# Graph stage in fewer tiles: block sums on VectorE, norms on GpSimd, and a permutation in two-byte parts

## The chip, the cores and the metric

One core of one Trainium2 chip runs the whole program in one launch. The metric is the device time in microseconds (us). Times of one instruction are in nanoseconds (ns). The engines are TensorE (PE, with its weight loads as PEld), VectorE (DVE), ScalarE (ACT), GpSimd (POOL) and SyncE (SP, here a queue for transfers).

## The reference

There are 32 graphs (B) of 512 nodes (N) with 64 features (D). Each passes through four steps with a residual and a normalisation after each. Cut to what matters:

```python
def reference(x, adj, nodemask, ...):
    # layer 0: messages = (A / clip(deg, 1)) @ x
    # layer 1: Chebyshev polynomials of the Laplacian, 4 orders, then a weight and a bias
    # layer 2: hyperbolic attention over all pairs of nodes (logmap, sigmoid, expmap, proj)
    # layer 3: dilate the adjacency, then for each node and feature a weighted
    #          sum of the 0.25, 0.5 and 0.75 quantiles over its neighbours,
    #          then a two-layer perceptron
    # between the layers: x = layernorm(x + layer(x)); a node mask of ones
    return x
```

The third layer is the unusual one: for each node, the values of its neighbours must be sorted, feature by feature. A node has at most 24 neighbours in the case that the fast path covers (K = 24).

## The kernel before, in words

**Lanes.** A graph goes through lanes: `front` (load, transposition of the adjacency, layers 0 and 1), `pairs` and `tail` (layer 2), `graph` (dilation, order of the nodes by their number of neighbours, and for each neighbour its slot), `gather` (one-hot matrices on DVE, with which PE picks neighbour values into sorting strips), `sort` (a sorting network on DVE over the strips `SB` and `SH`, then the weighted sum of ranks), and `head` (for each pair of graphs: the rest of the sort, the permutation back, layer 3's perceptron, the last norm and the store).

**The order.** The program records every operation with a planned duration and a lag (`seq.op`), and a planner, `Order.issue`, lays them out in time: each lane has a due time in units of a period of 80 us (`STAGES`), the ready operation with the earliest due time goes first, and on PE a change of matmul shape is weighed by `STAY`. The result is one fixed order for each engine. Where the plan leaves PE idle, filler matmuls (`stay_active`, L1453 and L1454) are put in to keep PE active. On the chip each engine takes its list in order and waits at each instruction for what it needs. `gp` is the helper for a small operation on POOL; it plans 1.0 us and a lag of 0.5. `rsqrt` raises to the power -0.5 on POOL (L722).

**The graph stage.** `graph` builds `nbT` (neighbours, f16, 128x2048), counts, and from it `v` and then `V`, all in the pool `gm` with one buffer each. `order` ranks the nodes, builds the permutation `perm` (L852, in the buffer of `nbT`), multiplies V by it into `VP` (L857, in the buffer of `v`), and forms prefix sums over the four row blocks of VP: block j takes j+1 matmuls (L863), 10 in all, and the column totals take 4 more (L867). All matmuls are recorded by one helper, line 502; DVE's by lines 448 (two tensors), 452 (tensor and scalars) and 455; ACT's by line 483. PSUM tiles of one lane come from `bank`, and the lane `graph` has one.

**The norms.** `layernorm` runs `bn_stats` and `bn_aggr` for four blocks on DVE (L714, L717), then variance plus epsilon, the power on POOL, an offset on DVE, and four ACT instructions that scale. It is called four times per graph: twice in `front`, once at the end of `tail` (on `v`, giving `x3`), and once in `dense` at the end of `head`.

**The permutation back.** `sort` and `head` leave the weighted sums in `ap` (f32, 128x512 for a pair of graphs). `finish` multiplies it by one-hot matrices `PT` in f32, which PE takes in two passes each: eight passes per graph. The last pair of graphs has its one-hot matrices made early (`spots`).

Of the kernel before, what the change touches and what calls it, by code (L numbers as in the profile page):

```python
# [8 lines left out]
F32 = mybir.dt.float32  # L9
# [11 lines left out]
P = 128  # L21
# [10 lines left out]
K = 24  # L32
# [148 lines left out]
class Order:  # L181
# [5 lines left out]
    HOP = 0.1  # L187
    STAY = 51.0

# [214 lines left out]
def tile_adj_resnorm(ctx: ExitStack, tc: tile.TileContext, x, adj, nodemask, w1k, b1k, att_w, att_b,  # L404
# [42 lines left out]
    def tt(out, a, b, op):  # L447
        vec(lambda: nc.vector.tensor_tensor(out, a, b, op=op), out, [a, b])  # L448
# [8 lines left out]
    def cp(out, a):  # L457
        vec(lambda: nc.vector.tensor_copy(out, a), out, [a], True)
# [7 lines left out]
    def gp(f, out, ins):  # L466

        seq.op("POOL", 1.0, 0.5, f, [out], ins)

# [140 lines left out]
    nc.vector.memset(tiny, 1e-36)  # L610
    onesb = const.tile([P, P], BF16, name="onesb")
    nc.vector.memset(onesb, 1.0)
    zero = const.tile([P, 2 * P], BF16, name="zero")
    nc.vector.memset(zero, 0.0)
# [104 lines left out]
    def rsqrt(v, name):  # L719

        y = col(name)
        seq.op("POOL", 0.8, 0.6, lambda: nc.gpsimd.tensor_tensor(y, v, mhalf, op=OP.pow), [y], [v])  # L722
        return y

    def layernorm(dst, z):

        st = seq.tile(pools["small"], [P, T, nc.vector.BN_STATS_DIM], F32, "st", 2)
        mv = seq.tile(pools["small"], [P, T, nc.vector.BN_AGGR_DIM], F32, "mv", 2)
        for t in range(T):
            bn_stats(st[:, t, :], z[:, t, :])  # L730
        for t in range(T):
            bn_aggr(mv[:, t, :], st[:, t, :])
        var = col("var")
        ts(var, mv[:, :, 1], EPS, None, op0=OP.add)
# [95 lines left out]
    def order(b, res):  # L830
# [17 lines left out]
        rkh = seq.tile(pools["keep"], [P, T], F16, "rkh", 8)  # L848
        cp(rkh, rk)
        perm = seq.tile(gm, [P, T, N], F16, "perm", 1, "nbT")  # L850
        for t in range(T):
            ts(perm[:, t, :], iotap, rk[:, t:t + 1], None, op0=OP.is_equal)  # L852
        VP = seq.tile(gm, [P, T, N], F16, "VP", 1, "v")
        for j in range(T):
            pt = bank()
            for t in range(T):
                mm(pt, V[:, t, j * P:(j + 1) * P], perm[:, t, :], start=(t == 0), stop=(t == T - 1))  # L857
            act(VP[:, j, :], pt, AF.Copy)
        slot = seq.tile(pools["keep"], [P, T, N], F16, "slot", 2)
        for j in range(T):  # L860
            pt = bank()
            for k in range(j + 1):
                mm(pt, UC[:, :P] if k == j else UC[:, P:2 * P], VP[:, k, :], start=(k == 0), stop=(k == j))  # L863
            act(slot[:, j, :], pt, AF.Copy)
        pt = bank()
        for k in range(T):
            mm(pt, onesP, VP[:, k, :], start=(k == 0), stop=(k == T - 1))  # L867
        if b % 2 == 0:
# [13 lines left out]
    def front(b, res):  # L882
# [38 lines left out]
        R = seq.tile(mid, [P, T, KO * D], F32, "R", 1)  # L921
        layernorm(R[:, :, :D], z)


        dm = col("dm")
        ts(dm, deg, 2e-35, None, op0=OP.max)
        dsc = rsqrt(dm, "dsc")
        pos = col("pos")
        ts(pos, deg, 0.0, None, op0=OP.is_gt)
        tt(dsc, dsc, pos, op=OP.mult)  # L930
        g = col("g")
# [22 lines left out]
        for t in range(T):  # L954
            mm(pt[:, t, :], onesb, bias1, start=True, stop=False)
            for u in range(nu):
                mm(pt[:, t, :], RT[:, u, t * P:(t + 1) * P], wk[:, u, :], start=False, stop=(u == nu - 1))

        FL = FLS[:, b % 2]
        var, rs = layernorm(FL[:, :, :D], pt[:, :, :D])  # L960
        tt(FL[:, :, D + 2:D + 7:4], pt[:, :, D:], bc(rs, 2), op=OP.mult)

# [6 lines left out]
    def pairs(b, res):  # L969
# [128 lines left out]
        q = rowsum(x2, S, "xs")  # L1098
        stt(s1, q, -2.0, s1, op0=OP.mult, op1=OP.add)
        tt(s1, s1, hh, op=OP.mult)  # L1100
        u = wide("u")
# [168 lines left out]
    def head(b, res):  # L1270
# [19 lines left out]
        for g in range(2):  # L1290
            mm(pt[P - CUT:, g * P:(g + 1) * P], PRS[:, g:g + n - 1:2], identf, start=True, stop=True)
        act(ap[P - CUT:, :, 1, :], pt[P - CUT:, :2 * P].rearrange("p (g c) -> p g c", g=2), AF.Copy)
        for g in range(2):
            finish(b - 1 + g, res["ends"][g], ap[:, g], res["spots"][g] if b == B - 1 else None)

    def spots(ends):
# [3 lines left out]
        home = seq.tile(mid, [P, 4, N], F32, "ends", 1, "Q")  # L1300
        ones = [seq.tile(mid, [P, 4, N], F32, f"ones{g}", 1, tag) for g, tag in enumerate(("EX", "RW"))]
        seq.lane = "tail"
# [12 lines left out]
    def finish(b, end, ap, spot):  # L1315
        rk, x3 = end
        if spot:
            ones, home = spot
            po = bank(home=home and "pairs")
            for u in range(2):  # L1320
                for h in range(2):
                    mm(po[h * D:(h + 1) * D, :], ap[:, u, h * D:(h + 1) * D], ones[:, 2 * h + u], start=(u == 0),
                       stop=(u == 1 and h == 1), pair=True)
# [11 lines left out]
        for u in range(2):  # L1335
            PT = seq.tile(pools["fin"], [P, 2, N], F32, "PT", 1)
            for h in range(2):
                onehot(PT[:, h, :], rr, nposc[:, 2 * h + u:2 * h + u + 1], pools["fin"])
            for h in range(2):
                mm(po[h * D:(h + 1) * D, :], ap[:, u, h * D:(h + 1) * D], PT[:, h, :], start=(u == 0),  # L1340
                   stop=(u == 1 and h == 1), pair=True)
        for t in range(T):
# [3 lines left out]
    def dense(po, x3T, x3, dst, nm, home=None):  # L1346
# [14 lines left out]
        for t in range(T):  # L1361
            mm(py[:, t, :], onesb, bias2, start=True, stop=False)
            mm(py[:, t, :], hT[:, t * P:(t + 1) * P], w2s, start=False, stop=True)
# [6 lines left out]
    flag = const.tile([1, 1], I32, name="flag")  # L1370
    limits = const.tile([B, 2, K + 1], F32, name="limits")
    for s in range(K + 1):
# [11 lines left out]
    def within_bounds():  # L1384
# [17 lines left out]
        for i, op in enumerate((OP.is_gt, OP.is_lt)):  # L1402
# [11 lines left out]

    STAGES = {"front": (-0.6, -0.5), "pairs": (1.2, 1.3), "tail": (0.2, 1.5), "graph": (0.9, 1.0), "gather": (2.7, 2.9),
              "sort": (4.5, 4.6), "head": (4.7, 5.6), "ends": (4.0, 4.5), "check": (3.4, 4.8)}

    nc.scalar.preload_act_table_set("natural_log_exp_and_others")
    with ExitStack() as fast:
# [31 lines left out]
        def stay_active():  # L1451
            if seq.open:
                return nc.tensor.matmul(PA[:, 2 * P:], zero[:, :P], zero, start=False, stop=False)  # L1453
            return nc.tensor.matmul(PA[:, 2 * P:], identb, UC[:, :2 * P], start=True, stop=True)  # L1454
# [250 lines left out]
```

## Time and profile before

| | |
|---|---|
| time, median of 3 runs | 2621.71 us (2621.48 to 2628.53) |
| profiled execution | 2622.02 us, span 2620.2 us |
| granted TensorE clock | 0.982 |
| busy: PE, DVE, ACT, POOL | 2458.2, 2402.7, 1879.2, 815.8 us |
| chain that ended last | DVE 72%, PE 18%, ACT 6%, issue 2%, POOL 2% |
| transfers | 49.96 MB, 19 GB/s over the span |

The span runs from the first to the last instruction. "Busy" is the time in which at least one instruction of the engine runs; PE's includes the filler. A group's row gives line, engine, operation, tile written and tiles read, shapes and count, then busy time in us and mean duration in ns, then the idle time of the engine just before and what ended it. A wait's row gives the waiting instruction, the releaser, total us, times, and the longest.

### The profile page before, as it was taken

The numbers are of one execution on the slowest core, as the hardware profiler recorded it, in microseconds if no ns is written. First come the engines' busy times: TensorE is split into PE (matmuls) and PEld (weight loads), VectorE is DVE, ScalarE is ACT, GpSimd is POOL, SyncE is SP. The second block draws the span as 40 slices with busy tenths as digits, with TensorE's granted clock in tenths as the row PEclk, the third lists the DMA queues.
The fourth block names the chain that finished last, engine by engine and source line by source line (L and its number), as shares of the span: only waits on it lengthen the run. The fifth ranks groups of instructions, "written<-read, shape, count | busy, mean of one in ns | idle before, by whom it ended". The sixth has DMA issues, their size and how long they took to land.

```text
span 2620.2 us, 55667 instructions
## 1 busy us (share of the span) xinstructions
PE 2458.2 (94%) x19641; PEld 1635.4 (62%) x19667; DVE 2402.7 (92%) x9002; ACT 1879.2 (72%) x4406; POOL 815.8 (31%) x1783
## 2 busy tenths in 40 slices
PE   7999999999999999999999999999999999999997
PEld 6666566666666666666656666566666666666655
DVE  3668998999999999999999999999999999998996
ACT  5666677767777777767777677777777778776761
POOL 1233332332343333322333233333323333332210
PEclk9999999999999999999999899999999999998999
DMA  1100000000000000000000000000000000000000
GB/s 38 33 23 21 17 14 15 25 22 23 18 11 22 20 25 21 24 17 13 20 21 25 19 19 13 20 23 22 26 19 13 18 19 26 19 11 3 5 7 8
DMA packets 119723, 49.96 MB, mean 19 GB/s; under 512 B 53740, under 2 KB 119436, under 8 KB 119436
## 3 DMA queue, kind: packets, MB, share of 16 engines
q1 hardware_dynamic: 118272, 46.15, 6.4%
q8 instruction: 156, 2.56, 0.4%
q14 instruction: 131, 1.07, 0.1%
q10 hardware_dynamic: 1164, 0.18, 0.0%
HBM read 37.93 MB, written 8.39 MB: 18 GB/s over the span
## 4 chain that ended last, share of the span: by engine, by line
DVE 72%; PE 18%; ACT 6%; issue 2%; POOL 2%; DMA 0%; ACTq 0%; DVEq 0%
DVE SB L448 17%; DVE SH L448 8%; DVE gather_oh L452 6%; PE front_bank L502 5%; DVE pairs_Q L448 4%; PE gather_bank L502 3%; PE graph_bank L502 3%; DVE pairs_RW L448 3%; PE pairs_bank L502 3%; DVE sort_prod L448 3%; DVE pairs_Wt L455 3%; DVE pairs_L L455 2%; DVE tail_v L448 2%; DVE pairs_EX L448 2%; DVE pairs_RW L455 2%
## 5 line engine op out<-in xcount | busy, mean ns | idle before, releaser
L448 DVE TENSOR_TENSOR SB<-SB 128x448 f32<-128x448 f32 (+11 forms) x1424 | 565.8, 424 | 12.2 <-ACT SB L483 0.7
L502 PE MATMUL gather_bank<-gather_oh,tail_x3h 128*64 128x448 f16 (+5 forms) x5376 | 516.5, 321 | 4.8 <-ACT SB L483 3.4
L502 PEld LDWEIGHTS <-tail_x3h 128*64 128x64 bf16 x5376 | 296.0, 111 | 214.3 <-issue 112.8
L448 DVE TENSOR_TENSOR SH<-SH 128x32 f32<-128x32 f32 (+11 forms) x1744 | 347.4, 246 | 8.1
L502 PE MATMUL pairs_bank<-pairs_FT 67*128 67x512 f32 (+7 forms) x768 | 316.9, 516 | 18.7 <-ACT pairs_EX L483 7.1
L452 DVE TENSOR_SCALAR gather_oh<-graph_slot 128x256 f16<-128x256 f16 (+9 forms) x864 | 252.3, 337 | 25.3 <-PE gather_bank L502 23.5
L502 PE MATMUL front_bank<-front_AT,front_y 128*64 128x512 f32 x768 | 189.5, 607 | 18.5 <-DVE front_y L448 17.0
L502 PEld LDWEIGHTS pairs_bank<-pairs_FT 67*128 67x128 f32 (+1 forms) x768 | 130.2, 194 | 83.2 <-issue 19.7
L502 PE MATMUL graph_bank<-graph_perm,graph_V 128*128 128x512 f16 x512 | 141.0, 382 | 16.1 <-DVE graph_perm L452 13.8
L502 PEld LDWEIGHTS <-graph_nbT 128*128 128x128 f16 x1536 | 113.1, 99 | 57.6 <-issue 17.3
L722 POOL TENSOR_TENSOR front_rs<-front_var,mhalf 128x4 f32<-128x4 f32 x64 | 83.4, 1303 | 201.8 <-DVE front_var L452 152.9
L502 PEld LDWEIGHTS front_bank<-XA,front_AT 128*128 128x128 f32 x1024 | 126.0, 194 | 13.6 <-issue 6.3
L1453 PE MATMUL PA<-zero 128*128 128x256 bf16 x973 | 132.9, 278 | 0.1
L502 PE MATMUL pairs_bank<-FLS,pairs_Wt 128*128 128x66 f32 x1024 | 124.7, 274 | 3.9 <-DVE pairs_Wt L455 3.8
L502 PEld LDWEIGHTS pairs_bank<-FLS,pairs_Wt 128*128 128x128 f32 x1024 | 120.6, 192 | 10.9 <-DVE pairs_Wt L455 7.8
L502 PE MATMUL front_bank<-XA,front_AT 128*128 128x65 f32 x1024 | 124.5, 274 | 0.0
L448 DVE TENSOR_TENSOR pairs_RW<-pairs_RW,pairs_EX 128x640 f32<-128x640 f32 x128 | 104.1, 815 | 18.7 <-ACT pairs_RW L483 18.4
L502 PEld LDWEIGHTS <-tabs 128*128 128x128 f16 x1296 | 78.3, 100 | 64.2 <-issue 54.9
L502 PEld LDWEIGHTS front_bank<-front_AT,front_y 128*64 128x64 f32 x768 | 54.5, 137 | 95.6 <-issue 63.0
L483 ACT ACTIVATE graph_VP<-graph_bank 128x512 f16<-128x512 f32 x128 | 75.5, 590 | 53.7 <-PE graph_bank L502 49.4
L483 ACT ACTIVATE SB<-gather_bank 128x448 f32<-128x448 f32 (+2 forms) x192 | 81.3, 438 | 43.4 <-PE gather_bank L502 43.0
L502 PE MATMUL head_bank<-head_PT,sort_ap 128*64 128x512 f32 x240 | 111.2, 608 | 0.1
(354 smaller groups left out, 6569.8 us busy)
## 6 DMA issues: line engine op xcount, KB each, us to landing
front_A<-in_adj_dram SPq DMA_DIRECT2D x128, 256.0 KB, 2.7
XA<-in_x_dram SPq DMA_DIRECT2D x32, 128.0 KB, 2.2
xs<-tail_x SPq DMA_DIRECT2D x32, 128.0 KB, 1.9
out_dram<-head_zo SPq DMA_DIRECT2D x31, 128.0 KB, 2.0
out_dram<-tail_ends SPq DMA_DIRECT2D x1, 128.0 KB, 2.1
wk<-in_L_gnn_weight_dram ACTq DMA_DIRECT2D x1, 64.0 KB, 3.0
w1s<-in_L_gnn_W_dram ACTq DMA_DIRECT2D x2, 32.0 KB, 2.0
attw<-in_L_gnn_att_W_dram ACTq DMA_DIRECT2D x2, 0.2 KB, 3.2
```

The source lines that it names most:

```text
L448: vec(lambda: nc.vector.tensor_tensor(out, a, b, op=op), out, [a, b])
L452: vec(lambda: nc.vector.tensor_scalar(out, a, s1, s2, op0=op0, **kw), out, [a], True, (s1, s2))
L455: vec(lambda: nc.vector.scalar_tensor_tensor(out, a, s, b, op0=op0, op1=op1), out, [a, b], False, (s,))
L483: 0.3, lambda: nc.scalar.activation(out, a, f, scale=scale, **kw), [out, accum_out], [a, after] + sc, table)
L502: return nc.tensor.matmul(out, w, a, start=start, stop=stop)
L722: seq.op("POOL", 0.8, 0.6, lambda: nc.gpsimd.tensor_tensor(y, v, mhalf, op=OP.pow), [y], [v])
L1453: return nc.tensor.matmul(PA[:, 2 * P:], zero[:, :P], zero, start=False, stop=False)
```

## The change

It has these parts:

- `perm` stands in the buffer of `v`, and `VP` is written over `V` by column blocks, each seen as four strips of 128.
- The prefix sums over blocks are running sums on DVE (`sums`, three additions per graph, in the buffers of `junk` and of VP's own first blocks), so that block j takes at most two matmuls and the totals one.
- `layernorm` has a second form, the default, in which everything between `bn_stats` and the scaling runs on POOL; the two calls in `front` pass `soon=True` and keep the old form.
- Six or so small operations in `front`, `order` and `tail` move from DVE to POOL.
- `ap` is split into three bf16 parts whose sum it is (`aph`), the one-hot matrices are f16, and the permutation takes 12 two-byte matmuls per graph.
- The bias matmuls use the f16 ones instead of bf16 ones, the filler's moving operand is a broadcast column, and `limits` is f16.
- The planner's figures change: `STAY`, `STAGES`, the planned cost of `gp` and of `rsqrt`.

```diff
-    STAY = 51.0
+    STAY = 48.0
...
-        seq.op("POOL", 1.0, 0.5, f, [out], ins)
+        seq.op("POOL", 0.28, 0.25, f, [out], ins)
...
-    onesb = const.tile([P, P], BF16, name="onesb")
-    nc.vector.memset(onesb, 1.0)
-    zero = const.tile([P, 2 * P], BF16, name="zero")
+    zero = const.tile([P, P], BF16, name="zero")
...
-        seq.op("POOL", 0.8, 0.6, lambda: nc.gpsimd.tensor_tensor(y, v, mhalf, op=OP.pow), [y], [v])
+        seq.op("POOL", 1.1, 0.3, lambda: nc.gpsimd.tensor_tensor(y, v, mhalf, op=OP.pow), [y], [v])
...
-    def layernorm(dst, z):
+    def layernorm(dst, z, soon=False):
+        if not soon:
+            st = seq.tile(pools["small"], [P, T, nc.vector.BN_STATS_DIM], F32, "st", 2)
+            for t in range(T):
+                bn_stats(st[:, t, :], z[:, t, :])
+            off, even, var, d, odd, v = (st[:, :, i] for i in range(6))
+            gtt(d, even, odd, op=OP.subtract)
+            gtt(var, var, v, op=OP.add)
+            gts(d, d, 0.5, None, op0=OP.mult)
+            gts(var, var, 1.0 / D, EPS, op0=OP.mult, op1=OP.add)
+            gtt(d, d, d, op=OP.mult)
+            gtt(v, var, d, op=OP.add)
+            rs = rsqrt(v, "rs")
+            gtt(off, even, odd, op=OP.add)
+            gts(off, off, -0.5, None, op0=OP.mult)
+            gtt(off, off, rs, op=OP.mult)
+            for t in range(T):
+                act(dst[:, t, :], z[:, t, :], AF.Identity, bias=off[:, t:t + 1], scale=rs[:, t:t + 1])
+            return
...
-        cp(rkh, rk)
-        perm = seq.tile(gm, [P, T, N], F16, "perm", 1, "nbT")
+        gts(rkh, rk, 1.0, None, op0=OP.mult)
+        perm = seq.tile(gm, [P, T, N], F16, "perm", 1, "v")
...
-        VP = seq.tile(gm, [P, T, N], F16, "VP", 1, "v")
+        VP = [V[:, :, j * P:(j + 1) * P] for j in range(T)]
...
-            act(VP[:, j, :], pt, AF.Copy)
+            act(VP[j], four(pt), AF.Copy)
...
+        sums = [None, VP[0], four(seq.tile(gm, [P, N], F16, "sums", 1, "junk")), VP[0], VP[1]]
...
-            for k in range(j + 1):
-                mm(pt, UC[:, :P] if k == j else UC[:, P:2 * P], VP[:, k, :], start=(k == 0), stop=(k == j))
+            mm(four(pt), UC[:, :P], VP[j], start=True, stop=(j == 0))
+            if j:
+                mm(four(pt), UC[:, P:2 * P], sums[j], start=False, stop=True)
+                tt(sums[j + 1], sums[j], VP[j], op=OP.add)
...
-        for k in range(T):
-            mm(pt, onesP, VP[:, k, :], start=(k == 0), stop=(k == T - 1))
+        mm(four(pt), onesP, sums[T], start=True, stop=True)
...
-        layernorm(R[:, :, :D], z)
+        layernorm(R[:, :, :D], z, True)
...
-        ts(dm, deg, 2e-35, None, op0=OP.max)
+        gts(dm, deg, 2e-35, None, op0=OP.max)
...
-        ts(pos, deg, 0.0, None, op0=OP.is_gt)
-        tt(dsc, dsc, pos, op=OP.mult)
+        gts(pos, deg, 0.0, None, op0=OP.is_gt)
+        gtt(dsc, dsc, pos, op=OP.mult)
...
-        stt(s1, q, -2.0, s1, op0=OP.mult, op1=OP.add)
-        tt(s1, s1, hh, op=OP.mult)
+        gts(q, q, -2.0, None, op0=OP.mult)
+        gtt(s1, s1, q, op=OP.add)
+        gtt(s1, s1, hh, op=OP.mult)
...
+        aph = seq.tile(pools["fin"], [P, 3, 2, 2, P], BF16, "aph", 1)
+        for q in range(3):
+            act(aph[:, q], ap, AF.Copy)
+            if q < 2:
+                tt(ap, ap, aph[:, q], op=OP.subtract)
...
-            PT = seq.tile(pools["fin"], [P, 2, N], F32, "PT", 1)
+            PT = seq.tile(pools["fin"], [P, 2, N], F16, "PT", 1)
...
-            for h in range(2):
-                mm(po[h * D:(h + 1) * D, :], ap[:, u, h * D:(h + 1) * D], PT[:, h, :], start=(u == 0),
-                   stop=(u == 1 and h == 1), pair=True)
+            for q in range(3):
+                for h in range(2):
+                    mm(po[h * D:(h + 1) * D, :], ap[:, q, u, h * D:(h + 1) * D], PT[:, h, :], start=(u == 0 and q == 0),
+                       stop=(u == 1 and q == 2 and h == 1))
...
-    STAGES = {"front": (-0.6, -0.5), "pairs": (1.2, 1.3), "tail": (0.2, 1.5), "graph": (0.9, 1.0), "gather": (2.7, 2.9),
-              "sort": (4.5, 4.6), "head": (4.7, 5.6), "ends": (4.0, 4.5), "check": (3.4, 4.8)}
+    STAGES = {"front": (-1.0, 0.3), "pairs": (1.2, 1.3), "tail": (0.7, 1.2), "graph": (1.2, 1.3), "gather": (2.9, 3.0),
+              "sort": (4.3, 4.9), "head": (4.7, 5.6), "ends": (4.1, 4.4), "check": (2.9, 5.3)}
```

More of the change, by code (lines that the diff above doesn't have):

```diff
@@ L848, in order, with four @@
         rkh = seq.tile(pools["keep"], [P, T], F16, "rkh", 8)
-        cp(rkh, rk)
-        perm = seq.tile(gm, [P, T, N], F16, "perm", 1, "nbT")
+        gts(rkh, rk, 1.0, None, op0=OP.mult)
+        perm = seq.tile(gm, [P, T, N], F16, "perm", 1, "v")
         for t in range(T):
             ts(perm[:, t, :], iotap, rk[:, t:t + 1], None, op0=OP.is_equal)
-        VP = seq.tile(gm, [P, T, N], F16, "VP", 1, "v")
+        def four(a):
+            return a.rearrange("p (t n) -> p t n", n=P)
+        VP = [V[:, :, j * P:(j + 1) * P] for j in range(T)]
         for j in range(T):
@@ L954, in front @@
         for t in range(T):
-            mm(pt[:, t, :], onesb, bias1, start=True, stop=False)
+            mm(pt[:, t, :], onesP, bias1, start=True, stop=False)
             for u in range(nu):
@@ L959, in front @@
         FL = FLS[:, b % 2]
-        var, rs = layernorm(FL[:, :, :D], pt[:, :, :D])
+        var, rs = layernorm(FL[:, :, :D], pt[:, :, :D], True)
         tt(FL[:, :, D + 2:D + 7:4], pt[:, :, D:], bc(rs, 2), op=OP.mult)
@@ L1292, in head @@
         act(ap[P - CUT:, :, 1, :], pt[P - CUT:, :2 * P].rearrange("p (g c) -> p g c", g=2), AF.Copy)
+        aph = seq.tile(pools["fin"], [P, 3, 2, 2, P], BF16, "aph", 1)
[3 more added lines that the diff above has]
+                tt(ap, ap, aph[:, q], op=OP.subtract)
         for g in range(2):
-            finish(b - 1 + g, res["ends"][g], ap[:, g], res["spots"][g] if b == B - 1 else None)
+            finish(b - 1 + g, res["ends"][g], aph[:, :, g], res["spots"][g] if b == B - 1 else None)
     def spots(ends):
@@ L1300, in spots @@
         home = seq.tile(mid, [P, 4, N], F32, "ends", 1, "Q")
-        ones = [seq.tile(mid, [P, 4, N], F32, f"ones{g}", 1, tag) for g, tag in enumerate(("EX", "RW"))]
+        ones = [seq.tile(mid, [P, 4, N], F16, f"ones{g}", 1, tag) for g, tag in enumerate(("EX", "RW"))]
         seq.lane = "tail"
@@ L1320, in finish @@
             for u in range(2):
-                for h in range(2):
-                    mm(po[h * D:(h + 1) * D, :], ap[:, u, h * D:(h + 1) * D], ones[:, 2 * h + u], start=(u == 0),
-                       stop=(u == 1 and h == 1), pair=True)
+                for q in range(3):
+                    for h in range(2):
+                        mm(po[h * D:(h + 1) * D, :], ap[:, q, u, h * D:(h + 1) * D], ones[:, 2 * h + u],
+                           start=(u == 0 and q == 0), stop=(u == 1 and q == 2 and h == 1))
             for t in range(T):
@@ L1335, in finish @@
         for u in range(2):
-            PT = seq.tile(pools["fin"], [P, 2, N], F32, "PT", 1)
+            PT = seq.tile(pools["fin"], [P, 2, N], F16, "PT", 1)
             for h in range(2):
                 onehot(PT[:, h, :], rr, nposc[:, 2 * h + u:2 * h + u + 1], pools["fin"])
-            for h in range(2):
-                mm(po[h * D:(h + 1) * D, :], ap[:, u, h * D:(h + 1) * D], PT[:, h, :], start=(u == 0),
-                   stop=(u == 1 and h == 1), pair=True)
+            for q in range(3):
+                for h in range(2):
+                    mm(po[h * D:(h + 1) * D, :], ap[:, q, u, h * D:(h + 1) * D], PT[:, h, :], start=(u == 0 and q == 0),
+                       stop=(u == 1 and q == 2 and h == 1))
         for t in range(T):
@@ L1361, in dense @@
         for t in range(T):
-            mm(py[:, t, :], onesb, bias2, start=True, stop=False)
+            mm(py[:, t, :], onesP, bias2, start=True, stop=False)
             mm(py[:, t, :], hT[:, t * P:(t + 1) * P], w2s, start=False, stop=True)
@@ L1370, in tile_adj_resnorm @@
     flag = const.tile([1, 1], I32, name="flag")
-    limits = const.tile([B, 2, K + 1], F32, name="limits")
+    limits = const.tile([B, 2, K + 1], F16, name="limits")
     for s in range(K + 1):
@@ L1452, in stay_active @@
             if seq.open:
-                return nc.tensor.matmul(PA[:, 2 * P:], zero[:, :P], zero, start=False, stop=False)
+                return nc.tensor.matmul(PA[:, 2 * P:], zero, zero[:, 0:1].to_broadcast([P, 2 * P]), start=False, stop=False)
             return nc.tensor.matmul(PA[:, 2 * P:], identb, UC[:, :2 * P], start=True, stop=True)
```

## The prediction

> **What bounds the kernel now.** I read the page first: busy shares, then the 40 slices.
>
> ```profile
> PE 2458.2 (94%) x19641; PEld 1635.4 (62%) x19667; DVE 2402.7 (92%) x9002; ACT 1879.2 (72%) x4406; POOL 815.8 (31%) x1783
> DVE  3668998999999999999999999999999999998996
> ```
>
> VectorE (DVE) and TensorE (PE) both look full, ScalarE has a quarter of its time left and GpSimd (POOL) two thirds. The chain that ended last settles which is first: the page gives it as DVE 72%, PE 18%, ACT 6%. Next I split the span into fill, middle and drain, and asked for the same stretches of L1453 alone, the filler matmul that only keeps PE awake.
>
> ```profile
> 0.00:131.00 131.00, 113.89 (x881) 84.99 (x882) 64.95 (x266) 79.38 (x158) 24.32 (x128) 1.00 0.13 36
> 131.00:262.00 131.00, 124.39 (x978) 86.74 (x977) 99.95 (x318) 88.63 (x214) 47.26 (x107) 0.96 0.08 22
> 262.00:2560.00 2298.00, 2174.77 (x17393) 1429.62 (x17418) 2199.16 (x8236) 1701.65 (x4012) 741.19 (x1546) 0.98 0.07 18
> 2560.00:2620.20 60.20, 45.17 (x396) 34.08 (x396) 38.68 (x183) 9.55 (x24) 2.99 (x3) 0.92 0.04 9
> ```
>
> Columns are PE, PEld, DVE, ACT, POOL busy. DVE idles 131-64.95 = 66.1 us, then 31.1, then 98.8, then 21.5: together 217.5, and 2402.7+217.5 is the span, 2620.2. So time = DVE work + those four idles. In the middle only about 63 of PE's 2175 us are filler (58.9 from L1453, 4.3 from L1454), so PE is loaded with real work at 92% there against DVE's 96%. What ends DVE's waits in the middle:
>
> ```profile
> DVE gather_oh L452 <- PE gather_bank L502: 19.5, 14, 3.0
> DVE pairs_RW L448 <- ACT pairs_RW L483: 12.7, 12, 3.7
> DVE front_st L714 <- PE front_bank L502: 9.7, 23, 2.3
> DVE head_off L455 <- POOL head_rs L722: 2.1, 3, 0.9
> ```
>
> Summing that list by releaser: PE 48 us, ACT 20, POOL 7; some 24 lie in gaps too small for it.
>
> **What the skill says, against this trace.** "SBUF — State Buffer", section "Who interferes with whom", says that a VectorE instruction with two SBUF inputs, or in a two-port mode, excludes a GpSimd instruction that reads SBUF: whichever came second waits. A stretch of the timeline shows who pays here:
>
> ```profile
> 1007.54 0.15 DVE L455 SCALAR_TENSOR_TENSOR front_off<-front_mv,front_rs 128x4 f32<-128x4 f32 x1
> 1007.61 0.17 DVE L448 TENSOR_TENSOR FLS<-front_bank,front_rs 128x8 f32<-128x8 f32 x1
> ...
> 1009.43 0.49 POOL L471 TENSOR_TENSOR pairs_hx<-pairs_hh,FLS 128x4 f32<-128x4 f32 x1
> 1009.78 1.28 DVE L455 SCALAR_TENSOR_TENSOR pairs_Wt<-pairs_bank,pairs_Q 128x512 f32<-128x512 f32 x2
> 1009.88 0.20 POOL L471 TENSOR_TENSOR pairs_hb<-pairs_hh,FLS 128x4 f32<-128x4 f32 x1
> ```
>
> POOL needs 0.20 us while DVE reads PSUM, 0.49 while DVE sorts in SBUF. DVE shows nothing: its 128x448 sort step takes 616 ns with no POOL instruction beside it and 619 with one (178 and 174 of them, sorted so from the timeline). I go by the trace: more POOL work costs POOL time, DVE 3 ns per instruction at worst. "VectorE: DVE Perf Modes" (Mode 2×_1P) gives `tensor_tensor` two results a cycle for packed 16-bit operands of step one. The trace agrees: 414 ns for 512 f16 elements, 683 for 512 f32. It also shows the f16 price with rows of 128 at a stride (the diagonal of nbT), the layout of the new block sums.
>
> ```profile
> L448 DVE TENSOR_TENSOR graph_nbT<-graph_nbT,identb 128x512 f16<-128x512 f16 x32 | 13.2, 414 | 0.1
> L448 DVE TENSOR_TENSOR PRS<-PRS 128x512 f32<-128x512 f32 x16 | 10.9, 683 | 0.1
> L717 DVE BATCH_NORM_AGGREGATE tail_mv<-tail_st 128x2 f32<-128x6 f32 x128 | 11.5, 150 | 0.0
> L502 PE MATMUL head_bank<-head_PT,sort_ap 128*64 128x512 f32 x240 | 111.2, 608 | 0.1
> L502 PE MATMUL graph_bank<-graph_VP,UC 128*128 128x512 f16 x320 | 91.2, 383 | 2.6 <-ACT graph_VP L483 1.9 <-ACT graph_slot L483 0.5
> ```
>
> **The ledger of DVE.** Back-to-back DVE instructions overlap by about 80 ns (1007.54, 0.15 long, next at 1007.61), so an instruction occupies its duration minus 0.08.
> Added: three f16 block sums per graph, 96 x (0.414-0.08) = +32.1 us. Splitting `ap` in three: two f32 subtractions per pair of graphs, 32 x (0.683-0.08) = +19.3.
> Removed: in `layernorm` without `soon` (tail and dense, 64 calls) four aggregates each, 256 x 0.07 = -17.9 (four in a row took 0.36 us in the drain: (0.36-0.15)/3); the variance and offset instructions, 128 x 0.077 = -9.9. The rank cast, dm, pos, dsc*pos and two of s1 (rows of 139 to 161 ns), 192 x 0.075 = -14.4.
> Net +51.4-42.2 = **+9.2 us**. Taking whole durations instead, without overlap, would give a small gain; the overlap is visible, so I keep +9.
>
> **PE.** Slot prefix sums go from ten matmuls per graph to seven, totals from four to one: 96 x 0.285 (91.2/320) + 96 x 0.259 (33.1/128 on the totals' row) = -52 us. The final permutation was eight f32 passes per graph, 111.2 us for 30 graphs; it becomes 12 two-byte matmuls. If their halves run side by side as gather's do (188.6/1536 = 0.123 for 448 columns, so 0.140 for 512), 360 x 0.140 = 50 us, saving 61; if none pair, 101, saving 10. I take -113 in all, bounds -62 and -113. That is 5% of real PE work. The edits of the filler, the bias ones and the limits change an operand's source or type, not its columns: zero; a slower broadcast would lie in the filler's own 147 us.
>
> **ACT and POOL.** ACT gets three 128x512 copies per pair, 48 x 0.63 (the PT row) = +30 us, 73% busy: hidden by its own idle time in the middle (596 us); uncovered, 30. POOL gets 9 x 64 + 32 + 96 + 96 = 800 small instructions, 0.20 to 0.49 us, 0.35 as now on average: +280 us, 42% busy. Latency of a moved norm: aggregates, variance, power and offset took about 0.36+0.16+1.0+0.15 us; now nine POOL steps of 0.2 to 0.5 and the same power, 2.8 to 5.5. In the middle the wait hides behind other graphs' sort; x3 is then late by 1 to 4 us, and next gather's matmuls, which the order starts a graph or more later. DVE no longer waits for rs in tail and head: -3.5 us (2.1 + 1.4). Behind a late norm on POOL's queue stand the PAD memsets and the next pair's scalars, which 1557 us of POOL idle in the middle cover. SP's loads and stores are unchanged except that an output store follows its norm.
>
> **Buffers.** nbT is released after V instead of after the permutation; v after VP instead of after the totals; V is held until the totals. Next graph's v can start earlier, its V not before the totals. In the middle nbT waited 0.4 us in all, so there is little to free; a V that waits for the totals would stall ACT, which has slack; zero, bounds -5 and +10. Behind a sum that waits for its ACT copy, everything on DVE waits: rival 3.
>
> **Planned order.** POOL's planned cost falls from 1.0+0.5 to 0.28+0.25 us per step, near the 0.20 to 0.49 measured. The old figure put reciprocals too late in DVE's order; POOL then sat waiting:
>
> ```profile
> 78.95 0.20 POOL L471 TENSOR_TENSOR pairs_gam<-pairs_gam,pairs_dn 128x4 f32<-128x4 f32 x1 [7.37 <-DVE pairs_dn L461]
> 151.41 0.29 POOL L471 TENSOR_TENSOR tail_al<-tail_al,tail_y 128x4 f32<-128x4 f32 x1 [8.69 <-DVE tail_y L461]
> ```
>
> In the first graph that delays the gather that DVE idles for. Of these 16 us I take 12 off the fill; bounds 0 and 25. The shifted stage due times I cannot price; they move the middle's idle either way, 20 us.
>
> **Drain.** The last pair's `ap` passes three ACT copies and two DVE subtractions before the permutation: 3 x 0.63 + 2 x 0.68 + hops, 4 to 5 us, and the last norm +1; its matmuls give 1 back. +5.
>
> **The sum.** DVE 2402.7+9.2 = 2411.9. Fill 97.2-12 = 85. Middle 98.8, less half of the 48 that PE causes (5% less PE work, and PE the later only part of the time: my choice), less 3.5: 71. Drain 26.5. Span 2594.4; 1.8 lie outside it (2622.02 against 2620.2), so 2596. The profiled execution is 0.3 us above the median of 2621.71, so no correction: **2596, -1.0%**.
>
> **Rivals.**
> 1. PE was the true holder: all 48 us of waits vanish and the fill gives 25. 2411.9+72+47+26 = 2557, +1.8 = 2559. For it: PE 92% with real work. Against: DVE heads the chain with 72%.
> 2. The ledger only: PE's relief becomes filler, the fill stays. 2411.9+97.2+95.3+26.5 = 2631, so 2633, slightly slower. For it: DVE idles only 4% in the middle, so there is little to win, while its work rises.
> 3. Slower: the sums stall DVE. `graph_bank` has one buffer; a sum placed right behind its VP copy waits for ACT's 0.59 us copy. 96 x 0.59 = 57, giving 2653. It decides from 26/96 = 0.27 us a sum on. For it: gather_oh already waits 1.4 us a time. Against: graph_v, in a like place, waits only 1.4 us in the whole middle.
> That the norms' work is not really taken from DVE can be left out: BN aggregates would still be listed.
>
> **Chances.** A measurement of this kernel tells 0.3% (8 us) from no change. Forecast 0.50, rival 1 0.20, rival 2 0.16, rival 3 0.14. Faster takes most of the first two, 0.67; same 0.11, from the forecast's upper and rival 2's lower edge; slower 0.22. The range 2550 to 2650 leaves out the tails of rivals 1 and 3; the forecast's own is 2572 to 2616.
>
> **What would show it.** DVE busy 2405 to 2418; no BN aggregates under tail and head; a sums row near 414 ns, x96; PE without filler near 2200; POOL near 1100; DVE's idle in the middle near 70 and in the fill near 85. Wrong if the middle's idle stays at 99 (rival 2), if sums' rows carry idle of 25 us or more (rival 3), or if DVE's total falls by over 10.

## The result and the profile after

The changed kernel takes 2657.28 us, the median of 4 runs (2651.29 to 2661.67); the kernel before takes 2624.84 us in the same comparison (2621.48 to 2628.53). The ratio is 1.0122, with a 95% interval of 1.0095 to 1.0149: slower by 1.2%, where 1.0% faster was forecast. The profiled execution took 2661.67 us, its span is 2659.8, and the granted PE clock was 0.965 (0.982 before).

First the page of the changed kernel, its busy shares and VectorE's row of the 40 slices:

```profile
PE 2446.7 (92%) x19514; PEld 1627.0 (61%) x19514; DVE 2412.1 (91%) x8553; ACT 1918.0 (72%) x4470; POOL 1097.4 (41%) x2583
...
DVE  3668999999999999999899989999998999999995
```

DVE's work came out where the ledger put it: 2412.1 us, forecast 2411.9. POOL too: 1097.4, forecast about 1100. DVE's row looks much as before, with three 8s in the middle for two. The same four stretches as before (fill, fill, middle, last 60 us; columns PE, PEld, DVE, ACT, POOL busy, then the granted clock, the DMA share and GB/s):

```profile
0.00:131.00 131.00, 115.64 (x865) 87.26 (x866) 65.08 (x257) 77.82 (x148) 30.71 (x145) 0.97 0.12 33
131.00:262.00 131.00, 127.18 (x961) 85.04 (x959) 97.56 (x282) 93.37 (x223) 47.91 (x131) 0.93 0.09 25
262.00:2599.80 2337.80, 2161.61 (x17340) 1422.20 (x17339) 2216.54 (x7861) 1735.78 (x4076) 1009.25 (x2278) 0.97 0.07 18
2599.80:2659.80 60.00, 42.30 (x356) 32.50 (x354) 32.90 (x155) 11.00 (x25) 9.52 (x30) 0.88 0.04 9
```

Stretch minus DVE busy gives DVE's idle time:

| us | before | forecast | after |
|---|---|---|---|
| DVE busy | 2402.7 | 2411.9 | 2412.1 |
| idle, fill (two stretches) | 97.2 | 85 | 99.4 |
| idle, middle | 98.8 | 71 | 121.3 |
| idle, last 60 us | 21.5 | 26.5 | 27.1 |
| span | 2620.2 | 2594.4 | 2659.8 |

So the forecast missed the span by 65: 50 in the middle, 14 in the fill, and next to nothing in DVE's work and the drain. What ends DVE's waits in the middle (us in total, times, longest):

```profile
DVE tail_rem L448 <- ACT tail_x3h L483: 43.6, 19, 4.3
...
DVE front_st L712 <- PE front_bank L502: 16.2, 32, 1.6
...
DVE gather_oh L452 <- PE gather_bank L502: 7.1, 12, 2.2
```

The first row is new, and its 43.6 us are most of the 50 missed in the middle. Summed by releaser, PE causes 40.7 us (48.2 before, where the forecast took half of it away), ACT 50.9 (19.7), POOL 8.1 (6.8). `tail_rem` is `x3` minus its bf16 part, right behind the norm of a tail. ACT and PE in the same stretch say why ACT is late, and who else is:

```profile
ACT tail_x L483 <- POOL tail_st L471: 83.4, 26, 7.0
...
PE gather_bank L502 <- ACT SB L483: 24.2, 15, 5.3
```

The same two waits in the profile before:

```profile
ACT tail_x L483 <- DVE tail_off L455: 32.1, 22, 3.8
...
PE gather_bank L502 <- ACT SB L483: 3.4, 7, 0.9
```

ACT waits 83.4 us for the last GpSimd step of the tail's norm; before, the same instruction waited 32.1 us, for DVE. Behind it on ACT's queue stand copies that PE needs: PE's wait for one of them was 3.4 us before and is 24.2 now. The groups of after:

```profile
L471 POOL TENSOR_TENSOR tail_st<-tail_st 128x4 f32<-128x4 f32 x160 | 107.1, 690 | 103.9 <-DVE tail_st L712 95.2 <-DVE SH L448 4.0 <-DVE graph_c L452 2.5
...
L502 PE MATMUL head_bank<-head_PT,head_aph 128*64 128x512 f16 x360 | 85.3, 387 | 2.8 <-ACT head_PT L483 2.8
...
L502 PE MATMUL graph_bank<-graph_V,UC 128*128 128x512 f16 x192 | 63.7, 386 | 2.1 <-ACT graph_V L483 1.7 <-ACT graph_slot L483 0.3
...
L471 POOL TENSOR_TENSOR head_st<-head_st 128x4 f32<-128x4 f32 x160 | 52.4, 346 | 152.0 <-DVE head_st L712 148.1 <-DVE front_off L455 1.7 <-DVE pairs_hh L452 0.8
...
L448 DVE TENSOR_TENSOR graph_sums<-graph_V 128x512 f16<-128x512 f16 x32 | 13.3, 415 | 4.2 <-ACT graph_V L483 4.2
L448 DVE TENSOR_TENSOR graph_V<-graph_V 128x512 f16<-128x512 f16 x32 | 13.3, 415 | 0.1
L448 DVE TENSOR_TENSOR graph_V<-graph_sums,graph_V 128x512 f16<-128x512 f16 x32 | 13.2, 412 | 1.0 <-PE graph_bank L502 1.0
```

A norm step with two tensors takes 690 ns on GpSimd in the tail and 346 in the head, against 0.20 to 0.49 us assumed. The block sums cost what was said (412 to 415 ns) and stall DVE by 5.3 us in all. The final permutation fell from 111.2 to 85.3 us on PE, the slot sums and totals from 124.3 to 88.2 (63.7, and two rows of 12.4 and 12.1 that are not shown).

One norm from the timeline of after (start, duration, engine; in brackets the wait before it):

```profile
1314.62 1.79 POOL L471 TENSOR_TENSOR tail_st<-tail_st 128x4 f32<-128x4 f32 x3 [2.76 <-DVE tail_st L712]
...
1316.50 6.54 POOL L475 TENSOR_SCALAR tail_st<-tail_st 128x4 f32<-128x4 f32 x3
...
1323.01 0.48 POOL L471 TENSOR_TENSOR tail_st<-tail_st 128x4 f32<-128x4 f32 x2
...
1323.57 1.03 POOL L720 TENSOR_TENSOR tail_rs<-tail_st,mhalf 128x4 f32<-128x4 f32 x1
...
1324.92 1.43 ACT L483 ACTIVATE tail_x<-tail_v,tail_st,tail_rs 128x64 f32<-128x64 f32 x4 [6.00 <-POOL tail_st L471]
...
1326.88 0.22 PE L502 MATMUL front_bank<-bias,onesP 128*128 128x66 bf16 x1 [5.38 <-ACT front_RT L483]
...
1327.17 0.42 DVE L448 TENSOR_TENSOR tail_rem<-tail_x,tail_x3h 128x256 f32<-128x256 f32 x1 [4.21 <-ACT tail_x3h L483]
```

The chain starts at 1314.62 and ends at 1324.9. ACT stands for 6.00 us with the copy of `front_RT` behind it, so PE stands for 5.38; then DVE stands for 4.21 at `tail_rem`. All three wait for one late norm, since each runs its instructions in the written order. The mean over the 32 graphs in the trace is 6.9 us from the first step of the tail's norm to the end of its last (3.9 to 10.3), and 5.3 for the head's. The planner had counted about 4.2: nine steps of 0.28, a power of 1.1, and lags.

PE's standstill has a sequel. The stretches around it, with the granted clock as the third number from the end:

```profile
1317.40:1320.80 3.40, 3.40 (x41) 2.93 (x41) 3.40 (x10) 1.51 (x4) 3.40 (x1) 1.00 0.00 0
1320.80:1324.20 3.40, 0.70 (x14) 0.36 (x11) 2.16 (x11) 0.00 (x0) 3.08 (x6) 1.00 0.00 0
1324.20:1327.60 3.40, 0.72 (x7) 0.72 (x6) 0.43 (x2) 2.68 (x7) 0.60 (x2) 0.50 0.08 19
...
1331.00:1334.40 3.40, 3.40 (x20) 2.24 (x21) 2.88 (x16) 1.27 (x3) 1.25 (x1) 0.50 0.00 0
```

While PE stands, the clock is still full; it halves after 3.4 us with PE busy for 0.70 us, and stays at half for 10.2 us, in which PE works again. The trace of after has 31 such half-clock stretches, 187 us in all, and before has 14 with 97 us. Each of the 45 follows 3.4 us in which PE was busy for at most 87%, though many lulls of that size are followed by none. So here the standstill comes first, and the lower clock second.

### The profile page after: what moved, and what is told of

It reads as the page before. It is cut to its first block, busy times and chain, and to the rows that moved or that the text cites. A ratio compares the mean times of both kernels' runs of the same rounds, so it can differ in the third digit from the quotient of the medians.

```text
span 2659.8 us, 55854 instructions
## 1 busy us (share of the span) xinstructions
PE 2446.7 (92%) x19514; PEld 1627.0 (61%) x19514; DVE 2412.1 (91%) x8553; ACT 1918.0 (72%) x4470; POOL 1097.4 (41%) x2583
## 5 line engine op out<-in xcount | busy, mean ns | idle before, releaser
L502 PE MATMUL gather_bank<-gather_oh,tail_x3h 128*64 128x448 f16 (+5 forms) x5376 | 546.7, 328 | 24.3 <-ACT SB L483 24.2
L448 DVE TENSOR_TENSOR SH<-SH 128x128 f32<-128x128 f32 (+10 forms) x1744 | 352.7, 246 | 6.5
L483 ACT ACTIVATE graph_V<-graph_bank 128x512 f16<-128x512 f32 x256 | 151.1, 590 | 83.9 <-PE graph_bank L502 79.3
L471 POOL TENSOR_TENSOR tail_st<-tail_st 128x4 f32<-128x4 f32 x160 | 107.1, 690 | 103.9 <-DVE tail_st L712 95.2
L502 PE MATMUL pairs_bank<-FLS,pairs_Wt 128*128 128x66 f32 x1024 | 131.4, 275 | 1.4 <-DVE pairs_Wt L455 1.2
L483 ACT ACTIVATE graph_v<-graph_bank,graph_c 128x512 f16<-128x512 f32 x128 | 87.7, 685 | 62.3 <-PE graph_bank L502 56.8
L1182 POOL MEMSET SB<- 128x10 f32 (+2 forms) x96 | 14.0, 148 | 283.2 <-DVE SB L448 268.5
L502 PEld LDWEIGHTS front_bank<-XA,front_AT 128*128 128x128 f32 x1024 | 120.6, 192 | 5.8 <-issue 2.0
L1486 PE MATMUL PA<-zero 128*128 128x256 bf16 x870 | 119.2, 280 | 0.0
```

Of the source, the lines that this page charges most:

```text
L471: gp(lambda: nc.gpsimd.tensor_tensor(out, a, b, op=op), out, [a, b])
L483: 0.3, lambda: nc.scalar.activation(out, a, f, scale=scale, **kw), [out, accum_out], [a, after] + sc, table)
L502: return nc.tensor.matmul(out, w, a, start=start, stop=stop)
L1182: seq.op("POOL", 0.3, 0.3, lambda d=d: nc.gpsimd.memset(d, PAD), [d], [])
L1486: return nc.tensor.matmul(PA[:, 2 * P:], zero, zero[:, 0:1].to_broadcast([P, 2 * P]), start=False, stop=False)
```

## The experiments

Theory A: the norms' chain on GpSimd runs longer than planned, and what stands behind its consumer in order pays. Rival B: the changed planned costs and stages laid a worse order. Rival C: the lower granted clock is itself the cause. Theory D: the ledger alone, with little to gain from PE's relief. DVE busy and idle times below are of the profiled executions; ratios are to the kernel before on the same chip.

**e1 and e2: norms back on DVE, in the changed kernel.** The last argument selects the old path; so that it fits in memory, `st` has one buffer outside of front, and variance and offset are written in place in `mv`. What these narrower tiles cost by themselves (in e1, e2 and e6) no run tells.

```diff
-        layernorm(x3, v)
+        layernorm(x3, v, True)
```

> The changed kernel, with only the tail's norm back in its old form on VectorE (its small tiles are narrower, to fit). Theory A (the tail's norm is starved on GpSimd, and ScalarE and VectorE stand in order behind it): the 44 us for which tail_rem waited on VectorE go, 14 us of VectorE work come back, so about 2625 us, and the waits of ScalarE for tail_st (83 us) go with them. Rival B (the planner's new figures gave a worse order): no gain, 2650 to 2670. Rival C (the lower granted TensorE clock, 0.965 for 0.982, is the cause): the clock stays and the time with it.

For e2 also `layernorm(z, z)` to `layernorm(z, z, True)`.

> The changed kernel with both norms, of tail and head, back on VectorE. Theory A: the head's norm was not starved (346 ns a step against 690 in the tail), so beside the run with the tail's alone this costs 14 us more VectorE work and wins only the 16 us for which ScalarE waited on head_st: 2625 to 2640 us. Rival B: 2650 to 2670. If both norms mattered alike: below 2615.

**e3: the tail's norm planned as late as it is.** Only the planned lag of its last step is changed, from 0.25 to 5 us.

```diff
-            gtt(off, off, rs, op=OP.mult)
+            seq.op("POOL", 0.28, 5.0 if seq.lane == "tail" else 0.25,
+                   lambda: nc.gpsimd.tensor_tensor(off, off, rs, op=OP.mult), [off], [off, rs])
```

> The changed kernel; the tail's norm stays on GpSimd, but the plan gives its last step a lag of 5 us, so that what needs it stands later in the order of ScalarE and VectorE. Theory A, in the form that the loss is in the order behind a late result and not in GpSimd's own time: tail_rem's waits fall from 44 us to under 10 and the time to about 2620 us. If the starved steps cost something by themselves (port, GpSimd's queue): no gain, over 2645.

**e4: planned costs and stages alone,** in the kernel before. The later kernels that start from the kernel before contain this edit.

```diff
-    STAY = 51.0
+    STAY = 48.0
...
-        seq.op("POOL", 1.0, 0.5, f, [out], ins)
+        seq.op("POOL", 0.28, 0.25, f, [out], ins)
```

(and `rsqrt`'s costs and `STAGES`, as in the change.)

> The kernel before with only the planner's figures of the change: STAY, STAGES, and the planned cost of a GpSimd step and of the power. Theory A: 2605 to 2635 us, since nothing is on GpSimd that was not. Rival B: 2645 us or more, all of the loss. The prediction's own step (better figures shorten the fill): about 2610.

| | median us | ratio, 95% interval | DVE busy | DVE idle |
|---|---|---|---|---|
| changed kernel | 2657.28 | 1.0122 [1.0095, 1.0149] | 2412.1 | 247.7 |
| e1 | 2643.79 | 1.0077 [1.0048, 1.0106] | 2425.9 | 213.9 |
| e2 | 2639.09 | 1.0062 [1.0042, 1.0081] | 2437.2 | 195.4 |
| e3 | 2638.77 | 1.0059 [1.0030, 1.0088] | 2414.8 | 224.1 |
| e4 | 2621.26 | 0.9999 [0.9985, 1.0014] | 2405.4 | 209.2 |

e4 rules out B: the planned costs and stages by themselves move nothing. e1 gives DVE 14 us more work and is still faster than the changed kernel, since its idle time falls by 34; e2 adds 11 and loses another 18. e3 keeps the work where it is and only lets the planner know, and its idle time falls by 24. e1 and e3 end some 19 us above what theory A expected of them (2625 and 2620), so the late norm explains about half of the loss here. DVE's wait in e3:

```profile
DVE tail_rem L448 <- ACT tail_x3h L483: 5.4, 3, 2.6
```

Of 43.6 us, 5.4 are left, and PE's wait for the copy of `SB` is back from 24.2 us at 4.5 (2.8 in e1). What e2 and e3 leave, some 0.6%, has another cause (e12 below).

**e5 to e8: each part alone,** on top of e4. e5: the tiles of the permuted graph, the block sums, seven and one matmuls.

```diff
-            for k in range(j + 1):
-                mm(pt, UC[:, :P] if k == j else UC[:, P:2 * P], VP[:, k, :], start=(k == 0), stop=(k == j))
+            mm(four(pt), UC[:, :P], VP[j], start=True, stop=(j == 0))
+            if j:
+                mm(four(pt), UC[:, P:2 * P], sums[j], start=False, stop=True)
+                tt(sums[j + 1], sums[j], VP[j], op=OP.add)
```

> The kernel before with the planner's figures and only the graph stage's part: perm in v, VP over V, block sums on VectorE. Theory D (VectorE's own work decides, and relief of TensorE is worth little): VectorE's busy time rises by 32 us over the 2405 of the planner-only run, its idle falls by at most 10, about 2640 us. If TensorE's relief pays (the prediction): idle falls by 30 or more, about 2620.

e6: the final permutation in three bf16 parts, with the f16 one-hots, the smaller filler tile and the narrower small tiles that make room for them.

```diff
+        for q in range(3):
+            act(aph[:, q], ap, AF.Copy)
+            if q < 2:
+                tt(ap, ap, aph[:, q], op=OP.subtract)
```

> The kernel before with the planner's figures and only the permutation back in three bf16 parts (and the f16 ones, the smaller filler tile and narrower small tiles, without which it does not fit). Theory D: VectorE's work up by 19 us, idle down by at most 10: about 2633 us. If TensorE's relief pays: 2615 or less.

e7: both norms on GpSimd, nothing else (`layernorm` as in the change; `True` in front only).

> The kernel before with the planner's figures and only the two norms on GpSimd. Theory A (starvation of the tail's steps): VectorE's work falls by 28 us to about 2377, and its idle rises by 30 to 50, most of it tail_rem waiting for ScalarE: 2620 to 2640 us. If the norms did no harm: 2593.

e8: the head's norm and the small operations (`rkh`, `dm`, `pos`, `s1`) on GpSimd, the tail's norm on DVE.

```diff
-        cp(rkh, rk)
+        gts(rkh, rk, 1.0, None, op0=OP.mult)
...
-        layernorm(x3, v)
+        layernorm(x3, v, True)
```

> The kernel before with the planner's figures, the head's norm and the small operations of the change on GpSimd; the tail's norm, the prefix sums and the permutation back stay as before. Theories A and D together: VectorE's work falls by 28 us to about 2377 with the idle of the planner-only run, 209: about 2588 us, faster than both. If any step on GpSimd starves: idle above 225 and no gain over 2610.

| on top of e4 | median us | ratio, 95% interval | DVE busy | DVE idle |
|---|---|---|---|---|
| e5, sums | 2626.89 | 1.0047 [1.0029, 1.0066] | 2426.4 | 194.7 |
| e6, three parts | 2635.26 | 1.0064 [1.0038, 1.0089] | 2424.0 | 214.2 |
| e7, both norms | 2663.91 | 1.0189 [1.0169, 1.0209] | 2389.7 | 270.5 |
| e8, head norm and small | 2619.29 | 0.9997 [0.9978, 1.0015] | 2383.0 | 230.1 |

The norms alone lose more than the whole change. e7 takes 16 us of work off DVE and gives it 61 us of idle time, more than the 30 to 50 expected. Its waits in the middle show the same two rows:

```profile
ACT tail_x L483 <- POOL tail_st L471: 47.3, 21, 5.5
DVE tail_rem L448 <- ACT tail_x3h L483: 28.4, 20, 3.8
```

The head's norm does no harm (e8), though its steps are slowed too (381 ns); what comes after it feeds only an output, which may be why. It brings nothing either: DVE has 22 us less to do and idles 21 more. Sums and split lose about as theory D says: in e5 DVE gains 21 us of work and loses 14 of waiting, in e6 it gains 19 and loses none. The parts do not add up to the whole: e5, e6 and e7 multiply to 1.030, and the change took 1.012. Every edit lays the whole order anew, so no difference of half a per cent between two edits can be put down to one engine without a second sign.

**e9: e7 with the lag of e3.**

```diff
+            seq.op("POOL", 0.28, 5.0 if seq.lane == "tail" else 0.25,
```

> The norms-only kernel (2664 us), with a planned lag of 5 us after the last step of the tail's norm. Theory A' (the harm is done by what stands in order behind the late norm): tail_rem's waits fall from 28 us to under 8 and the time to about 2620 us. Theory A'' (the starved steps hurt by themselves): 2645 us or more.

Measured: 2628.85 us, 1.0011 [0.9985, 1.0037]; DVE busy 2388.1, idle 240.9. Its waits:

```profile
ACT tail_x L483 <- POOL tail_st L743: 6.9, 4, 3.6
DVE tail_rem L448 <- ACT tail_x3h L483: 6.0, 5, 2.9
```

The norms still take 6.8 us (up to 13.5), and of the 1.9% of loss all but 0.1% is gone: what cost the most was that the plan did not know the length. The length is not free either: against e4, DVE has 17 us less to do and idles 32 more.

**e10 and e11: what PE's relief is worth.** e10 is e4 with a final permutation of the first bf16 part alone.

```diff
+        aph = seq.tile(pools["fin"], [P, 1, 2, 2, P], BF16, "aph", 1)
+        act(aph[:, 0], ap, AF.Copy)
```

> The kernel before with the planner's figures; the permutation back takes only the first of the three bf16 parts of ap, without the two subtractions, so that two thirds of its precision are left out: TensorE's work falls by some 80 us in that group's row, VectorE's stays at 2405. The prediction's step (TensorE's relief removes half of the waits that it causes): idle falls from 209 us by 20 to 25, about 2592 us. Theory D (relief of TensorE alone is worth little): idle falls by under 10, 2610 us or more. If TensorE were the true holder: 2560.

e11 is e10 with e8's moves.

> As the run with less TensorE work (the same parts of ap left out), and also the head's norm and the small operations on GpSimd, which took 22 us off VectorE and gave nothing by themselves. Theory E (both engines are near full, and relief of one turns into its idle time unless the other is relieved too): about 2575 us, more than the sum of the two alone. If relief of VectorE is lost to GpSimd's late answers instead: idle stays at 230, about 2610.

The permutation's group on PE, in e4:

```profile
L502 PE MATMUL head_bank<-head_PT,sort_ap 128*64 128x512 f32 x240 | 114.6, 629 | 0.0
```

and in e10:

```profile
L502 PE MATMUL head_bank<-head_PT,head_aph 128*64 128x512 f16 x120 | 43.4, 398 | 0.7 <-ACT head_PT L483 0.6
```

e10 measured 2608.73 us, 0.9937 [0.9915, 0.9959]: 71 us less in the row bring 0.63% or 16.5 us, 0.23 per us (0.15 to 0.31 over the interval), with DVE's work unchanged (2405.5). e11 measured 2591.62, 0.9882 [0.9831, 0.9934]: the same moves that bring nothing in e8 bring about another 17 us here by medians, though the two intervals overlap a little. DVE's figures give the second sign: from e10 to e11 its work falls by 29 us and its idle time rises by 9, where in e8 all but 1 of 22 us came back as idle time. That fits two engines, each full enough to hold the other up; that the new order has a part in it is not ruled out.

**e12: what is left when the two losers go.** The tiles and sums, the head's norm and the small operations; the tail's norm stays on DVE and the permutation in f32. So e12 is e1 without the split and without what came with it (narrow tiles, and the edits of filler, bias ones and limits).

> The change without its two dearest parts, as a version to beat both: planner's figures, tiles and block sums, the head's norm and the small operations on GpSimd, but the tail's norm on VectorE and the permutation back in f32. VectorE 2383 + 21 = 2404 us, TensorE's rows 36 us lighter. Theory E: idle 195 to 200, about 2603 us, faster than before by 0.5%. If the gains don't add: 2615 to 2625.

Measured: 2605.31 us, 0.9940 [0.9911, 0.9969], faster than the kernel before by 0.6%, and by medians 1.8 to 2.0% faster than the changed kernel (0.9940/1.0122; 2605.31/2657.28). Its page:

```profile
PE 2431.6 (94%) x19354; PEld 1600.5 (62%) x19371; DVE 2407.3 (93%) x8714; ACT 1896.1 (73%) x4424; POOL 943.8 (36%) x2295
```

DVE has as much to do as before, but idles only 190.2 us, 71.4 of them in the middle. That is the number that the prediction gave for the whole change, but by luck, since this is another kernel. Again two parts that bring nothing alone (e5 loses, e8 is even) gain together: one relieves PE, and the other makes up for DVE's added work. Beside e1, e12 tells what the split costs in the changed kernel: from 1.0077 to 0.9940, with intervals that do not meet. Without it DVE has 19 us less to do, as priced, and idles 24 us less.

**e13 to e16: the norm's steps measured by themselves.** These kernels compute no part of the reference: a chain of 40 dependent GpSimd steps on 128x4 runs alone, then beside streams of one kind of DVE instruction.

```diff
+    phase("alone", lambda: None, 0)
+    phase("psum", lambda: nc.vector.tensor_tensor(b, bank[:, :448], a, op=OP.add), 60)
+    phase("sbuf", lambda: nc.vector.tensor_tensor(b, a, b, op=OP.max), 60)
```

> A kernel that leaves out the whole computation (it copies x to the output) and measures one thing: 40 dependent GpSimd steps of 128x4, four times, beside 60 back-to-back VectorE instructions each time: none; 448 elements with one operand in PSUM; 448 elements with two in SBUF; 1792 f16 elements with a scalar. If the busy VectorE starves GpSimd[...]: about 200 ns a step in the first two stretches, 400 ns or more in the last two, single steps of over 1 us. If the long steps in the kernel had another cause (queue, semaphores): 200 ns in all four.

In e13 the stretches ran into each other, so a chain partly ran beside the next stream; it decides nothing. e14 is the same with each stretch waiting for both engines.

> The same measurement with the four stretches held apart by data (in the first version VectorE's instructions of one stretch ran on into the next); the whole computation is left out again. If the busy VectorE starves GpSimd[...]: about 200 ns a step alone and beside the PSUM operand, 400 ns or more beside two SBUF operands and beside the f16 scalar form. If the long steps had another cause: 200 ns in all four.

```profile
L40 POOL TENSOR_TENSOR sbuf_q<-sbuf_q,s 128x4 f32<-128x4 f32 x40 | 23.3, 584 | 3.1
L40 POOL TENSOR_TENSOR mode_q<-mode_q,s 128x4 f32<-128x4 f32 x40 | 10.5, 262 | 3.1
L40 POOL TENSOR_TENSOR psum_q<-psum_q,s 128x4 f32<-128x4 f32 x40 | 8.0, 199 | 3.1
L40 POOL TENSOR_TENSOR alone_q<-alone_q,s 128x4 f32<-128x4 f32 x40 | 7.9, 198 | 3.1
...
L55 DVE TENSOR_TENSOR b<-a,b 128x448 f32<-128x448 f32 x60 | 37.5, 626 | 2.0
L54 DVE TENSOR_TENSOR b<-bank,a 128x448 f32<-128x448 f32 x60 | 37.4, 624 | 2.0
```

A step takes 198 ns alone, 199 while DVE reads one operand from PSUM, 584 while it reads both from SBUF: with the gap of 78 ns between steps (3.1 us over 40), one step for each DVE instruction. In the "mode" stretch, with a 16-bit compare, 7 DVE instructions overlapped the chain, and the steps beside them took up to 586 ns. DVE itself lost nothing (626 and 624).

e15 lets the DVE instructions run back to back on independent tiles, as they do in the kernel:

> The measurement of the small GpSimd steps once more (the whole computation left out), with one more stretch: VectorE instructions with two SBUF operands that don't depend on each other, four buffers in turn, so that each starts before the one before has ended, as in the kernel's own lists. If GpSimd gets in only between two VectorE instructions: there is no gap, and steps of several us appear, as in the changed kernel (three steps in 6.5 us). If a step gets in at every instruction whatever their overlap: 540 to 600 ns each, and the 6 us must have another cause.

```profile
L40 POOL TENSOR_TENSOR free_q<-free_q,s 128x4 f32<-128x4 f32 x40 | 18.5, 462 | 3.1
```

Still one step for each DVE instruction (537 ns from one to the next), 648 ns at most. e16 tries short instructions (128 elements), `scalar_tensor_tensor`, a mix as in the sort, and scalar compares, each as its own stream.

> The same small GpSimd steps (the whole computation left out) beside four other streams of VectorE: two SBUF operands of 128 elements; the form with a scalar and two tensors, 448 elements; a mix of that, of 448-element pairs and of the f16 scalar form; the f16 scalar form of 512 alone. If streaks of such forms shut GpSimd out, as the trace of the changed kernel suggests (a step let in only when VectorE next reads PSUM): steps of over 1 us here. If one step gets in at every instruction: none is longer than one VectorE instruction plus 200 ns.

No step took over 0.67 us in any of them. So the price of a step beside DVE is shown: 0.46 to 0.58 us for 0.20 beside 448-element instructions, 0.29 and 0.32 beside the short ones and the compares. The single steps of up to 5.9 us in the kernel are not: of the three steps from 1316.50 above, the first lasted 5.1 us, while DVE ran 16 instructions on SBUF in a row, and it ended when DVE next read PSUM, but no stream of e14 to e16 made a step much longer than one instruction. What makes those long stays open.

## Why the prediction was wrong, point by point

**The ledger of DVE: right in its sum.** +9.4 for +9.2. That is in part luck, for the parts alone were less exact and their errors cancel: sums +21.0 for 32.1 (e5), split +18.6 for 19.3 (e6), both norms -15.7 for -27.8 (e7).

**ACT and POOL: the first step that failed.** It read "In the middle the wait hides behind other graphs' sort; x3 is then late by 1 to 4 us", after a latency of "2.8 to 5.5". The tail's norm took 6.9 us, and the wait did not hide. The step asked what DVE could do meanwhile and not what stands behind the consumer on ACT: ACT waited 83.4 us, and copies for PE and `tail_rem` for DVE queued behind it. e7, e9, e3 and e1 show it from four sides. The profile before held the hint: at `tail_x` ACT already waited 32.1 us in the middle, so that path had no room for more latency.

**Planned order: wrong.** "near the 0.20 to 0.49 measured" took the steps in `pairs`, at their uncontended end, for the norms' steps (0.69 and 0.35). And the fill did not shrink: 99.4 for a forecast of 85, and in e4, where only the plan changes, 97.8. The 16 us of waits read from two lines of GpSimd were idle time of an engine that nobody waited for.

**PE and the split: mis-sized, the second step that failed.** The rows fell by 36 (slots, totals; 52 forecast) and 26 (permutation; 61 forecast, 10 as its lower bound), 62 in all, where 113 was taken; that this is the lower bound of the sum is chance. The halves of the permutation seldom paired: 55 of its 360 matmuls start within 50 ns of the one before, where gather has 2480 of 5376. And PE's work as a whole did not shrink: without filler it is 2311.7 us for 2311.2 before, with "near 2200" forecast, because other rows grew, gather's from 516.5 to 546.7 us. That came with the new plan: gather's row is 544.3 us in e4 already, at a clock of 0.983, and PE without filler 2343.8. The exchange rate was good: "half of the 48 that PE causes" for 113 us is 0.21 per us, and e10 measured 0.23. At that rate 62 us are worth 14 of gain, not 24; measured, the waits for PE fell by 7.5. So the split, priced at 19 us of DVE work for 61 us of PE's relief, brought 26 and lost (e6, and e1 against e12). By the prediction's own rate sums and split were a loss from the start, 51 us of DVE work for 24 us of waits: its gain had to come from the moves to GpSimd and from the fill, and neither gain came.

**Drain: right.** +5.6 for +5. **Rival 3: wrong.** The sums' rows carry 5.3 us of idle time, not 57. **Rival 1** fell with the waits for PE, 40.7 of 48.2 left. **Rival 2,** the ledger only, comes near what remains once the norm is planned: 1.0059 in e3 for its 1.004. e2's 1.0062 is like it in the number alone, for there DVE has 2437.2 us to do.

**The skill's rule.** "SBUF — State Buffer", section "Who interferes with whom", says that a DVE instruction with two SBUF inputs contends with a GpSimd instruction that reads SBUF, and that the order of issue decides which of the two waits, so that the step had its mechanism at hand. The prediction set against it that DVE does not pay, which held: in the trace of after the 128x448 sort step takes 619 ns with GpSimd work beside it (219 of them) and 616 without (133). What it left out is that GpSimd then pays at each of the ten steps of a norm.

**The clock, and what stays open.** The clock of the profiled executions is lower where there are more stalls (0.965 after, 0.969 in e7, 0.973 in e3, 0.975 in e9, 0.980 in e12, 0.982 before). The chain above shows one way from a stall to the clock. e3 and e9, which change nothing but a planned lag, win back time (half of the loss in e3, nearly all in e9) and raise the clock with it. So rival C does not stand as a cause of its own; nor did DVE's waits for PE grow in the changed kernel (40.7 us for 48.2). But time and clock go together closely. On one chip the kernel before itself ranges from 2609.74 us at 0.989 to 2639.57 at 0.973, about 19 us per 0.01. By that slope, as an estimate, the step from 0.982 to 0.965 would go with some 32 of the 40 us between the two profiled executions. How much of the loss is the waiting itself, and how much the slower matmuls after it, was not told apart. The loss left once the tail's norm is planned or moved back goes with the split (e1 and e12). Its 19 us of DVE work were priced; why DVE also idles 24 us more with it stays open.

## What to carry to other kernels

Where a chain moves to an idle engine, count its latency beside the busiest neighbour on the same memory, and then ask what stands in order behind its consumer on every engine; tell a planner that latency, or the queue will. Where two engines are both over 90% full, relief of one may bring little (0.23 us per us of PE here, nothing for DVE alone); relief of both brought more than the two apart in both pairs tried here, so edits are worth judging in pairs. Test the parts of a bundled change alone and in subsets: here two parts cost more than the whole, and the remaining ones beat the kernel before.

## What the runs showed of the hardware

Beside a stream of 448-element DVE instructions with two SBUF inputs, a chain of dependent GpSimd steps on 128x4 advanced at one step for each DVE instruction (198 ns alone, 462 or 584 beside such a stream, 199 beside one that reads PSUM), while DVE kept its own time (626 against 624 ns). In the changed kernel's trace, the 1602 of 2080 such steps that overlapped a DVE instruction with tensors in SBUF alone took 430 ns on average and up to 5.9 us, and the other 478 took 208 ns and at most 271. The steps of several microseconds were not reproduced alone. The granted clock of PE halved only behind 3.4 us in which PE was busy for at most 87%: in all 31 cases after and all 14 before.
